# A graph layer on one core: aggregation by seven products on 2x2 blocks instead of eight

## The chip, the core and the metric

The kernel runs on one NeuronCore of a Trainium2 chip. The core has five engines with a queue each: TensorE (PE in the profile, with its weight loads listed apart as PEld), VectorE (DVE), ScalarE (ACT), GpSimd (POOL) and SyncE (SP), which here only starts transfers. Data lies in HBM, in the on-chip memory SBUF (128 partitions) and in PSUM, which TensorE writes and which this kernel uses as eight banks of 128x512 float32. The metric is the device time of the whole kernel in microseconds (us), the median of the runs. Everything is float32.

## The reference, cut to what matters

The layer takes 32 graphs of 512 nodes ("tokens") with 256 channels and a 0/1 adjacency matrix for each. After a layer norm and a relu, each graph goes through two branches (a convolution over the tokens and a message passing) and a GRU gate. The change is in one line of the message passing, the product of the affinities `A` (512 x 512) with the messages `msg` (512 x 256):

```python
h = jnp.maximum(_layernorm(x, axis=-1), 0.0)          # the x below
s = x @ w_se.T + b_se                                 # 3 features of a node
sq = jnp.sum(s * s, axis=-1)
dist = sq[:, :, None] + sq[:, None, :] - 2.0 * jnp.einsum('bnd,bmd->bnm', s, s)
A = jnp.exp(-dist) * mask                             # mask is the adjacency
msg = jax.nn.relu(x @ w_msg.T + b_msg)
x_nmp = jnp.einsum('bnm,bmd->bnd', A, msg)            # the aggregation
# x_conv: 1x1 convolution, relu, 17-tap convolution, relu
x_in = jnp.concatenate([x_conv, x_nmp], axis=-1)
gi, gh = x_in @ w_ih.T + b_ih, x @ w_hh.T + b_hh      # then r, z, n, and the output
```

## The kernel before

The 32 graphs are worked in two groups of 16. For each group a first part normalises the graphs and takes them to the frequency domain (the 17-tap convolution is done there). Then `nodes` does the message passing of the 16 graphs, and in between the frequency products of the convolution (`product`, 40 units in each group, three 128x256 products of two channel chunks for a unit). After both groups a late part does the inverse transforms and the gates, which already use a scheme of seven products.

The messages of one graph, and one unit of the convolution:

```python
    def message(b):
        MSG[b] = pools["nodes"].tile([P, NC, D], FP, tag="msg", name=f"msg_{b}", bufs=3)
        ST[b] = pools["nodes"].tile([P, 2, NC, NS], FP, tag="st", name=f"st_{b}", bufs=2)
        hq = HQ.pop(b)
        h = N // D
        for c0 in range(0, NC, h):
            m = MSG[b][:, c0 : c0 + h, :]
            for j in range(h):
                c = c0 + j
                p = bank(f"pm_{b}_{c}")
                for ic in range(DC):
                    nc.tensor.matmul(p[:, : D + NS], hq[:, ic, c * P : (c + 1) * P], wmsg[:, ic, :],
                                     start=(ic == 0), stop=(ic == DC - 1))
                nc.vector.tensor_add(ST[b][:, 0, c, :], p[:, D : D + NS], bmsg[:, D:])
                nc.vector.tensor_add(m[:, j, :], p[:, :D], bmsg[:, :D])
            nc.scalar.activation(m, m, AF.Relu)
...
    def product(pw, g, u, xf):
        if u > 0 and (g, u) not in BOTH or (g, u) not in WT:
            prepare(pw, g, u, xf)
        wt = WT.pop((g, u))
        re, im = factors_of(xf, u)
        wr, wi = wt[:, 0], wt[:, 1]

        y = pw.tile([P, 2, D], FP, tag="y", name=f"y_{g}_{u}", bufs=3)
        p = bank(f"py_{g}_{u}")
        k1, k2 = p[:, :D], p[:, D:]
        if u == 0:
            terms = [(k1, re, wr), (k2, im, wi)]
        else:
            both, wsum = BOTH.pop((g, u)), WSUM.pop((g, u))
            k3 = bank(f"py2_{g}_{u}")[:, :D]
            terms = [(k3, both[:, 1], wr), (k2, both[:, 0], wi), (k1, re, wsum)]
        for dst, v, w in terms:
            for ic in range(DC):
                nc.tensor.matmul(dst, v[:, ic, :], w[:, ic, :], start=(ic == 0), stop=(ic == DC - 1))
        y_re, y_im = (by_half(y[:, k, :]) for k in range(2))
        if u == 0:
            nc.scalar.copy(y_re, halves(k1))
            nc.scalar.copy(y_im, halves(k2))
        else:
            nc.scalar.copy(y_im, halves(k1))
            nc.vector.tensor_sub(y_re, y_im, halves(k2))
            nc.vector.tensor_add(y_im, y_im, halves(k3))
        nc.scalar.dma_start(YD[g][:, 2 * u : 2 * u + 2, :], y)
```

The affinities and the aggregation. `ADJ` is turned in 32x32 blocks on VectorE; `A[b][:, mc, :]` is the chunk `mc` of 128 neighbours by 512 nodes. `aggregate` makes two outputs of 128 channels by 512 nodes, four matmuls each:

```python
    def affinity(b):

        A[b] = pools["nodes"].tile([P, NC, N], FP, tag="A", name=f"A_{b}", bufs=2)
        sl, sr = SL.pop(b), SR.pop(b)
        pd = [bank(f"pd_{b}_{mc}") for mc in range(NC)]
        for mc in range(NC):
            rows = slice(32 * mc, 32 * mc + 3 * NS)
            nc.tensor.matmul(pd[mc], sl[rows, :], sr[rows, :], start=True, stop=True)
        for mc in range(NC):
            e = pools["nodes"].tile([P, N], FP, tag="e", name=f"e_{b}_{mc}", bufs=2)
            nc.scalar.activation(e, pd[mc], AF.Exp)
            at = pools["nodes"].tile([P, N], FP, tag="at", name=f"at_{b}_{mc}", bufs=2)
            nc.vector.transpose(at.rearrange("p (j k) -> p j k", k=32), ADJ[b][:, :, 32 * mc : 32 * (mc + 1)])
            nc.vector.tensor_mul(A[b][:, mc, :], e, at)
        del ADJ[b]

    def aggregate(b, dcs=range(DC)):
        if 0 in dcs:
            NMP[b] = work.tile([P, DC, N], FP, tag="nmp", name=f"nmp_{b}")
        for dc in dcs:
            p = bank(f"pn_{b}_{dc}")
            for mc in range(NC):
                nc.tensor.matmul(p, MSG[b][:, mc, dc * P : (dc + 1) * P], A[b][:, mc, :],
                                 start=(mc == 0), stop=(mc == NC - 1))
            nc.scalar.copy(NMP[b][:, dc, :], p)
        if DC - 1 in dcs:
            del MSG[b], A[b]

    def save_nmp(b):
        nc.scalar.dma_start(ND[b], NMP.pop(b))
```

The loop over the graphs of a group. Outside the `manual_schedule` blocks a scheduler of the compiler decides the order on each engine from the order of recording and from the dependencies:

```python
        def nodes(g, xf, units, last):


            b1 = (g + 1) * GB
            todo = [b1 - 1] + list(range(g * GB, b1 - 1))
            def begin(i):
                if i < GB:
                    if todo[i] not in HQ:
                        by_chunks(todo[i])
                    message(todo[i])
                    features(todo[i])

            load_adj(todo[0])
            with tc.manual_schedule():
                begin(0)
                message(todo[1])
                factors(todo[0])
                features(todo[1])
            affinity(todo[0])
            for i, b in enumerate(todo):
                mine = spread(units, i, last) if i < last else []
                more = i + 1 < GB

                if g + 1 < NG and i == GB // 2:
                    load_x(b1)
                if g + 1 < NG and i == 3 * GB // 4:
                    statistics(b1)
                if i + 2 < GB and todo[i + 2] not in HT:
                    load_h(todo[i + 2])
                if more:
                    load_adj(todo[i + 1])
                    factors(todo[i + 1])

                parts = [range(DC)] if mine or not more else [[0], [1]]
                if len(parts) > 1:
                    aggregate(b, parts.pop(0))
                for u in mine[:1]:
                    product(pools["pw"], g, u, xf)
                begin(i + 2)
                if more:
                    affinity(todo[i + 1])
                for u in mine[1:2]:
                    product(pools["pw"], g, u, xf)
                aggregate(b, *parts)
                save_nmp(b)
                for u in mine[2:]:
                    product(pools["pw"], g, u, xf)
```

The beginning of the late part, which is recorded by hand: the loads of the first pair of graphs and of the combined gate weights go out from GpSimd's queue, and GpSimd then makes the sums of their blocks.

```python
    with phase("late"), phase("sw"), phase("ops", bufs=2), phase("work"), tc.manual_schedule():
        pairs = B // 2
        sw = pools["sw"].tile([P, K3, 7, 3, P], FP, name="sw")
        load_pair(0, nc.gpsimd)
        load_combined(sw, 0, 2)
        sums(HP[0], True)
        sums(NP[0], False)
        load_combined(sw, 2, 7)
        inverse(0)
        sums(CP[0], False)
...
def load_pair(p, queue=nc.sync):
    # yt, hp and np of the pair p: two hp loads, two yt loads, two np loads
def load_combined(sw, q0, q1):
    for k in range(K3):
        nc.gpsimd.dma_start(sw[:, k, q0:q1], WS[k][:, q0:q1])
```

## Time and profile before

| | us |
|---|---|
| device time, median of 3 runs | 1846.07 (1845.53 to 1846.49) |
| span of the profiled execution | 1848.1 |
| busy: PE / PEld / DVE / ACT / POOL | 1826.4 / 1089.0 / 1109.1 / 581.9 / 588.2 |
| aggregation matmuls (line 489), 512 records | 225.9 |
| products of affinity and mask on VectorE (line 480), 128 | 114.5 |
| frequency products (line 393), 952 records | 151.0 + 81.0 + 5.0 |
| messages (line 439), 512 records | 117.5 |

A line of the groups reads: source line, engine, operation, output<-inputs, shapes, count | time in which at least one of the group ran, mean of one in ns | idle time of the engine just before them, and what ended it. Matmuls overlap each other, so the mean of one (593 ns for 128x512) is longer than the distance between two; the distance is the busy time over the count. One float32 matmul leaves two records, so 512 records are 256 matmuls of the program. A line of the timeline reads: start, duration in us, engine, line, operation, names, shapes, count of merged instructions, and in brackets the idle time before it with what ended it. Times count from the start of the span.

### The profile page before, as it was taken

The numbers are of one execution on the slowest core, as the hardware profiler recorded it, in microseconds if no ns is written. First come the engines' busy times: TensorE is split into PE (matmuls) and PEld (weight loads), VectorE is DVE, ScalarE is ACT, GpSimd is POOL, SyncE is SP. The second block draws the span as 40 slices with busy tenths as digits, with TensorE's granted clock in tenths as the row PEclk, the third lists the DMA queues.
The fourth block names the chain that finished last, engine by engine and source line by source line (L and its number), as shares of the span: only waits on it lengthen the run. The fifth ranks groups of instructions, "written<-read, shape, count | busy, mean of one in ns | idle before, by whom it ended". The sixth has DMA issues, their size and how long they took to land.

```text
span 1848.1 us, 20105 instructions
## 1 busy us (share of the span) xinstructions
PE 1826.4 (99%) x6610; PEld 1089.0 (59%) x6610; DVE 1109.1 (60%) x2220; ACT 581.9 (31%) x1083; POOL 588.2 (32%) x572
## 2 busy tenths in 40 slices
PE   9999999999999999999999999999999999999998
PEld 6777666666888666665555554555455544555443
DVE  7775656554885555545266466655666466645666
ACT  4555434432335333333222221222122221222121
POOL 3331333333432344444422323133212322133221
PEclk9999999999999999999999999999999999999999
DMA  8999888875678887778421443234422442244312
GB/s 233 299 276 241 225 226 246 218 179 180 212 250 207 235 245 235 216 207 261 123 86 34 120 120 99 53 88 120 120 78 43 120 120 88 49 103 120 112 25 52
DMA packets 307452, 289.26 MB, mean 157 GB/s; under 512 B 148028, under 2 KB 237148, under 8 KB 306964
## 3 DMA queue, kind: packets, MB, share of 16 engines
q1 hardware_dynamic: 281300, 224.22, 46.0%
q10 hardware_dynamic: 19024, 38.68, 5.9%
q0 software_dynamic: 7024, 25.07, 4.8%
q8 instruction: 53, 0.87, 0.2%
q14 instruction: 51, 0.42, 0.1%
HBM read 191.50 MB, written 96.40 MB: 156 GB/s over the span
## 4 chain that ended last, share of the span: by engine, by line
PE 89%; DVE 4%; issue 3%; DMA 2%; POOL 1%; ACT 1%; SPq 0%; POOLq 0%; ACTq 0%; DVEq 0%
PE pg L597 29%; PE pn L597 14%; PE pn L489 11%; PE py L393 11%; PE pm L439 6%; PE pc L585 5%; PE pc L328 3%; PE px L343 3%; PE pw L256 2%; PE pd L474 2%; PE phT L312 1%; DMA w<-in_w_ihT_dram 1%; PE psr L463 1%; DVE stats L285 1%; DVE xn L304 1%
## 5 line engine op out<-in xcount | busy, mean ns | idle before, releaser
L489 PE MATMUL pn<-A,msg 128*128 128x512 f32 x512 | 225.9, 593 | 0.6 <-DVE A L480 0.6
L597 PE MATMUL pg<-hp,sw 128*128 128x512 f32 x434 | 221.8, 593 | 0.7 <-DVE rz L616 0.5
L597 PE MATMUL pg<-np,sw 128*128 128x512 f32 x434 | 221.6, 592 | 0.0
L597 PE MATMUL pg<-cp,sw 128*128 128x512 f32 x434 | 221.6, 592 | 0.0
L575 POOL TENSOR_TENSOR hp<-hp 128x512 f32<-128x512 f32 x64 | 81.3, 1280 | 413.0 <-DMA hp<-hd 234.6
L372 POOL TENSOR_TENSOR both<-xf 128x256 f32<-128x256 f32 x78 | 60.1, 771 | 329.1 <-PE py L393 297.5
L489 PEld LDWEIGHTS pn<-A,msg 128*128 128x128 f32 x512 | 97.2, 191 | 110.9 <-issue 105.7
L575 POOL TENSOR_TENSOR cp<-cp 128x512 f32<-128x512 f32 x64 | 80.4, 1267 | 229.8 <-ACT cp L591 228.6
L393 PE MATMUL py<-wt,both 128*128 128x256 f32 x624 | 151.0, 385 | 0.7 <-issue 0.7
L612 ACT ACTIVATE rz<-rz,brz 128x512 f32<-128x512 f32 x93 | 67.0, 721 | 260.2 <-DVE rz L616 260.2
L400 DVE TENSOR_TENSOR y<-y,py 128x256 f32<-128x256 f32 x78 | 31.8, 408 | 190.5 <-ACT y L399 185.8
L597 PEld LDWEIGHTS pg<-hp,sw 128*128 128x128 f32 x434 | 82.2, 190 | 104.8 <-issue 97.8
L597 PEld LDWEIGHTS pg<-cp,sw 128*128 128x128 f32 x434 | 82.5, 190 | 103.8 <-issue 103.8
L597 PEld LDWEIGHTS pg<-np,sw 128*128 128x128 f32 x434 | 82.5, 190 | 103.8 <-issue 103.8
L393 PEld LDWEIGHTS py<-wt,both 128*128 128x128 f32 x624 | 114.3, 190 | 43.2 <-issue 28.3
L480 DVE TENSOR_TENSOR A<-e,at 128x512 f32<-128x512 f32 x128 | 114.5, 933 | 36.9 <-ACT e L477 36.7
L359 POOL TENSOR_TENSOR wsum<-wt 128x512 f32<-128x512 f32 x78 | 109.1, 1399 | 51.8 <-DMA wt<-wd 39.1
L735 ACT ACTIVATE nt<-nt,vech 128x512 f32<-128x512 f32 x64 | 46.2, 722 | 235.8 <-DVE nt L734 235.8
L328 PE MATMUL pc<-w,hT 128*128 128x256 f32 x512 | 116.7, 381 | 1.6 <-DVE hT L316 1.6
L439 PE MATMUL pm<-wmsg,hq 128*128 128x259 f32 x512 | 117.5, 382 | 0.6 <-ACT sl L460 0.6
L597 PE MATMUL pn<-np,sw 128*128 128x512 f32 x224 | 114.4, 592 | 0.0
L597 PE MATMUL pn<-cp,sw 128*128 128x512 f32 x224 | 114.4, 592 | 0.0
(146 smaller groups left out, 2963.6 us busy)
## 6 DMA issues: line engine op xcount, KB each, us to landing
wt<-wd SPq DMA_DIRECT2D x160, 256.0 KB, 4.3
adj<-in_adj_dram SPq DMA_DIRECT2D x128, 256.0 KB, 5.4
wd<-wst SPq DMA_DIRECT2D x64, 320.0 KB, 5.3
yd<-y ACTq DMA_DIRECT2D x80, 256.0 KB, 4.3
yt<-yd SPq DMA_DIRECT2D x30, 640.0 KB, 7.5
hd<-hT SPq DMA_DIRECT2D x32, 512.0 KB, 4.4
nd<-nmp ACTq DMA_DIRECT2D x32, 512.0 KB, 4.0
xb<-in_x_dram SPq DMA_DIRECT2D x128, 128.0 KB, 3.8
```

Of the source, the lines that this page charges most:

```text
L328: nc.tensor.matmul(p[:, j, :], HT[b][:, ic, c * P : (c + 1) * P], w1[:, ic, :], start=(ic == 0), stop=(ic == DC - 1))
L343: nc.tensor.matmul(p[:, j * 2 * L : (j + 1) * 2 * L], H1[b][:, c0 + j, ic * P : (ic + 1) * P], fwd, start=True, stop=True)
L359: nc.gpsimd.tensor_tensor(t, WT[g, u][:, 0], WT[g, u][:, 1], op=ALU.add)
L372: nc.gpsimd.tensor_tensor(both[:, 0], re, im, op=ALU.add)
L393: nc.tensor.matmul(dst, v[:, ic, :], w[:, ic, :], start=(ic == 0), stop=(ic == DC - 1))
L439: nc.tensor.matmul(p[:, : D + NS], hq[:, ic, c * P : (c + 1) * P], wmsg[:, ic, :], start=(ic == 0), stop=(ic == DC - 1))
L480: nc.vector.tensor_mul(A[b][:, mc, :], e, at)
L489: nc.tensor.matmul(p, MSG[b][:, mc, dc * P : (dc + 1) * P], A[b][:, mc, :], start=(mc == 0), stop=(mc == NC - 1))
L575: nc.gpsimd.tensor_tensor(t[:, dst, :], t[:, a, :], t[:, b, :], op=sub)
L585: nc.tensor.matmul(bk[:, t0:t1], YT[p][j][:, c, oc * P : (oc + 1) * P], back[:, n : n + t1 - t0], start=(c == 0), stop=(c == len(spans) - ...
L597: nc.tensor.matmul(bk[:, t], sw[:, k, q, o, :], terms[k][q][:, t], start=(first and i == 0), stop=(i == len(ks) - 1), skip_group_check=True)
L612: nc.scalar.activation(rz[:, g, j, :], src, AF.Sigmoid, bias=brz[:, g : g + 1], scale=1.0)
```

## The change

The 512 neighbours, the 256 channels and the 512 nodes are each cut in two halves, so that one graph's aggregation is a product of 2x2 block matrices. Eight block products (each 128 channels by 256 neighbours by 256 nodes) become seven (Winograd's form of Strassen's scheme). For it four sums of message blocks are made on VectorE (`message_sums`, 128x256 each) and four sums of affinity blocks on GpSimd (`affinity_sums`, 128x512 each). Three PSUM banks gather the seven products; blocks that enter two outputs are copied out by ScalarE and added by VectorE. `aggregate` is now a generator in three pieces, between which other work of TensorE is recorded.

To make room in SBUF, the exponential goes straight into `A` (the tiles `e` are gone), and `at` and `sr` have one buffer instead of two. The load of the graph after next moves one step ahead, and at the start of a group the second half of one graph's messages moves behind the transposes of another. In the diff, `m[:, i, k]` is the block of messages with the half `i` of the channels and the half `k` of the neighbours, and `a[:, k, j]` the block of affinities with the half `k` of the neighbours and the half `j` of the nodes.

```diff
@@ -105,6 +105,7 @@
     def bank(name):
         return psum.tile([P, N], FP, tag="bank", name=name)
 
+    SM, TA = {}, {}
     X, ADJ, XN, HT, HQ, H1, MSG, A, NMP, ST, SL, SR = ({} for _ in range(12))
     XP, HP, NP, CP, YT, RZ, NT, OUT = ({} for _ in range(8))
 
@@ -425,12 +426,13 @@
             nc.scalar.copy(chunks(HQ[b][:, ic, :]), by_chunk(HT[b][:, ic, :]))
         del HT[b]
 
-    def message(b):
-        MSG[b] = pools["nodes"].tile([P, NC, D], FP, tag="msg", name=f"msg_{b}", bufs=3)
-        ST[b] = pools["nodes"].tile([P, 2, NC, NS], FP, tag="st", name=f"st_{b}", bufs=2)
-        hq = HQ.pop(b)
-        h = N // D
-        for c0 in range(0, NC, h):
+    def message(b, halves=range(2)):
+        if 0 in halves:
+            MSG[b] = pools["nodes"].tile([P, NC, D], FP, tag="msg", name=f"msg_{b}", bufs=3)
+            ST[b] = pools["nodes"].tile([P, 2, NC, NS], FP, tag="st", name=f"st_{b}", bufs=2)
+        hq = HQ[b]
+        h = NC // 2
+        for c0 in (h * k for k in halves):
             m = MSG[b][:, c0 : c0 + h, :]
             for j in range(h):
                 c = c0 + j
@@ -441,6 +443,8 @@
                 nc.vector.tensor_add(ST[b][:, 0, c, :], p[:, D : D + NS], bmsg[:, D:])
                 nc.vector.tensor_add(m[:, j, :], p[:, :D], bmsg[:, :D])
             nc.scalar.activation(m, m, AF.Relu)
+        if 1 in halves:
+            del HQ[b]
 
     def features(b):
 
@@ -461,7 +465,7 @@
         p = bank(f"psr_{b}")
         for c in range(NC):
             nc.tensor.transpose(p[:, c * P : (c + 1) * P], fr[:, c].rearrange("p g k -> p (g k)"), ident)
-        t = SR[b] = pools["nodes"].tile([P, N], FP, tag="sr", name=f"sr_{b}", bufs=2)
+        t = SR[b] = pools["nodes"].tile([P, N], FP, tag="sr", name=f"sr_{b}", bufs=1)
         nc.scalar.copy(by_chunk(t), chunks(p))
 
     def affinity(b):
@@ -473,24 +477,71 @@
             rows = slice(32 * mc, 32 * mc + 3 * NS)
             nc.tensor.matmul(pd[mc], sl[rows, :], sr[rows, :], start=True, stop=True)
         for mc in range(NC):
-            e = pools["nodes"].tile([P, N], FP, tag="e", name=f"e_{b}_{mc}", bufs=2)
-            nc.scalar.activation(e, pd[mc], AF.Exp)
-            at = pools["nodes"].tile([P, N], FP, tag="at", name=f"at_{b}_{mc}", bufs=2)
+            nc.scalar.activation(A[b][:, mc, :], pd[mc], AF.Exp)
+            at = pools["nodes"].tile([P, N], FP, tag="at", name=f"at_{b}_{mc}", bufs=1)
             nc.vector.transpose(at.rearrange("p (j k) -> p j k", k=32), ADJ[b][:, :, 32 * mc : 32 * (mc + 1)])
-            nc.vector.tensor_mul(A[b][:, mc, :], e, at)
+            nc.vector.tensor_mul(A[b][:, mc, :], A[b][:, mc, :], at)
         del ADJ[b]
 
-    def aggregate(b, dcs=range(DC)):
-        if 0 in dcs:
-            NMP[b] = work.tile([P, DC, N], FP, tag="nmp", name=f"nmp_{b}")
-        for dc in dcs:
-            p = bank(f"pn_{b}_{dc}")
-            for mc in range(NC):
-                nc.tensor.matmul(p, MSG[b][:, mc, dc * P : (dc + 1) * P], A[b][:, mc, :],
-                                 start=(mc == 0), stop=(mc == NC - 1))
-            nc.scalar.copy(NMP[b][:, dc, :], p)
-        if DC - 1 in dcs:
-            del MSG[b], A[b]
+
+
+
+    H2 = NC // 2
+
+    def message_sums(b):
+        m = MSG[b].rearrange("p (k c) (i d) -> p i k c d", k=2, i=DC)
+        (a11, a12), (a21, a22) = (m[:, 0, 0], m[:, 0, 1]), (m[:, 1, 0], m[:, 1, 1])
+        t = SM[b] = pools["nodes"].tile([P, 3, H2, P], FP, tag="sm", name=f"sm_{b}", bufs=1)
+        s1, s2, s4 = (t[:, k] for k in range(3))
+        nc.vector.tensor_add(s1, a21, a22)
+        nc.vector.tensor_sub(s2, s1, a11)
+        nc.vector.tensor_sub(a21, a11, a21)
+        nc.vector.tensor_sub(s4, a12, s2)
+
+    def affinity_sums(b):
+        m = A[b].rearrange("p (k c) (j n) -> p k j c n", k=2, j=2)
+        (b11, b12), (b21, b22) = (m[:, 0, 0], m[:, 0, 1]), (m[:, 1, 0], m[:, 1, 1])
+        t = TA[b] = pools["nodes"].tile([P, 3, H2, N // 2], FP, tag="ta", name=f"ta_{b}", bufs=1)
+        t1, t2, t4 = (t[:, k] for k in range(3))
+        sub = ALU.subtract
+        nc.gpsimd.tensor_tensor(t1, b12, b11, op=sub)
+        nc.gpsimd.tensor_tensor(t2, b22, t1, op=sub)
+        nc.gpsimd.tensor_tensor(b12, b22, b12, op=sub)
+        nc.gpsimd.tensor_tensor(t4, b21, t2, op=sub)
+
+    def aggregate(b):
+
+        m = MSG[b].rearrange("p (k c) (i d) -> p i k c d", k=2, i=DC)
+        a = A[b].rearrange("p (k c) (j n) -> p k j c n", k=2, j=2)
+        out = NMP[b] = work.tile([P, DC, N], FP, tag="nmp", name=f"nmp_{b}")
+        (s1, s2, s4), (t1, t2, t4) = ([t[:, k] for k in range(3)] for t in (SM[b], TA[b]))
+        lo, hi = slice(0, N // 2), slice(N // 2, N)
+
+        def into(bk, w, v, first):
+            for c in range(H2):
+                nc.tensor.matmul(bk[:, lo], w[:, c], v[:, c], start=(first and c == 0), stop=(c == H2 - 1), skip_group_check=True)
+
+        b1, b2, b3 = (bank(f"pn{k}_{b}") for k in range(3))
+
+        p1, u2, u3 = out[:, 1, lo], out[:, 0, hi], out[:, 1, hi]
+        into(b1, m[:, 0, 0], a[:, 0, 0], True)
+        nc.scalar.copy(p1, b1[:, lo])
+        into(b2, s2, t2, True)
+        nc.vector.tensor_add(u2, p1, b2[:, lo])
+        yield
+        into(b1, m[:, 0, 1], a[:, 1, 0], False)
+        nc.scalar.copy(out[:, 0, lo], b1[:, lo])
+        into(b2, m[:, 1, 0], a[:, 0, 1], False)
+        nc.vector.tensor_add(u3, p1, b2[:, lo])
+        into(b3, s1, t1, True)
+        nc.vector.tensor_add(out[:, 1, hi], u3, b3[:, lo])
+        yield
+        into(b2, m[:, 1, 1], t4, False)
+        nc.vector.tensor_add(out[:, 1, lo], p1, b2[:, lo])
+        into(b3, s4, a[:, 1, 1], False)
+        nc.vector.tensor_add(out[:, 0, hi], u2, b3[:, lo])
+        del MSG[b], A[b], SM[b], TA[b]
+        yield
 
     def save_nmp(b):
         nc.scalar.dma_start(ND[b], NMP.pop(b))
@@ -945,8 +996,9 @@
             load_adj(todo[0])
             with tc.manual_schedule():
                 begin(0)
-                message(todo[1])
+                message(todo[1], [0])
                 factors(todo[0])
+                message(todo[1], [1])
                 features(todo[1])
             affinity(todo[0])
             for i, b in enumerate(todo):
@@ -957,23 +1009,24 @@
                     load_x(b1)
                 if g + 1 < NG and i == 3 * GB // 4:
                     statistics(b1)
-                if i + 2 < GB and todo[i + 2] not in HT:
-                    load_h(todo[i + 2])
                 if more:
                     load_adj(todo[i + 1])
                     factors(todo[i + 1])
-
-                parts = [range(DC)] if mine or not more else [[0], [1]]
-                if len(parts) > 1:
-                    aggregate(b, parts.pop(0))
+                parts = aggregate(b)
+                message_sums(b)
+                affinity_sums(b)
                 for u in mine[:1]:
                     product(pools["pw"], g, u, xf)
                 begin(i + 2)
+                if i + 3 < GB:
+                    load_h(todo[i + 3])
+                next(parts)
                 if more:
                     affinity(todo[i + 1])
+                next(parts)
                 for u in mine[1:2]:
                     product(pools["pw"], g, u, xf)
-                aggregate(b, *parts)
+                next(parts)
                 save_nmp(b)
                 for u in mine[2:]:
                     product(pools["pw"], g, u, xf)
```

## The prediction

> **What bounds the kernel now.** I read the busy shares first, then the groups, then the timeline of TensorE in one loop of `nodes`, and last the other engines' timelines at the places where the change could make TensorE wait. From the page:
>
> ```profile
> span 1848.1 us, 20105 instructions
> PE 1826.4 (99%) x6610; PEld 1089.0 (59%) x6610; DVE 1109.1 (60%) x2220; ACT 581.9 (31%) x1083; POOL 588.2 (32%) x572
> ...
> PEclk9999999999999999999999999999999999999999
> ...
> L489 PE MATMUL pn<-A,msg 128*128 128x512 f32 x512 | 225.9, 593 | 0.6 <-DVE A L480 0.6
> ...
> L575 POOL TENSOR_TENSOR hp<-hp 128x512 f32<-128x512 f32 x64 | 81.3, 1280 | 413.0 <-DMA hp<-hd 234.6
> ```
>
> TensorE is busy 99% of the span at full clock, so every us of its work that goes is a us of the end, and every new wait of it is a us lost. The aggregation waited 0.6 us in all. Timeline of TensorE, one loop with three units:
>
> ```profile
> 741.40 7.03 PE L489 MATMUL pn<-A,msg 128*128 128x512 f32 x16
> 748.27 1.89 PE L393 MATMUL py<-wt,both 128*128 128x256 f32 x8
> 750.00 1.03 PE L393 MATMUL py<-wsum,xf 128*128 128x256 f32 x4
> 750.86 0.27 PE L458 MATMUL psl<-ident,fl 128*128 128x128 f32 x1
> ...
> 757.60 1.14 PE L474 MATMUL pd<-sr,sl 9*128 9x512 f32 x8
> ...
> 761.36 7.03 PE L489 MATMUL pn<-A,msg 128*128 128x512 f32 x16
> ```
>
> Starts matter here, not durations. Sixteen 512-column records take 748.27 - 741.40 = 6.87 us, 0.429 each; twelve 256-column records take 750.86 - 748.27 = 2.59 us, 0.216 each. So halving the columns costs next to nothing per record (0.432 for two against 0.429). A loop lasts 19.96 us without a gap. Busy time in such a stretch, columns as in the page (PE, PEld, DVE, ACT, POOL, clock, DMA share, GB/s):
>
> ```profile
> 780.00:800.00 20.00, 20.00 (x83) 13.65 (x83) 10.77 (x28) 7.44 (x16) 8.59 (x9) 1.00 0.77 221
> ```
>
> VectorE has 9 us of room in 20, GpSimd 11.
>
> **What the Trainium skill says.** (1) "TensorE: Matmul & The Clock Gate", Back-to-back issue gap, gives N/2.4 + 2.5 ns for N columns: 109 ns for 256 and 216 for 512. The 216 and 429 ns here are twice 108 and 215, so one record holds two passes; the trace agrees. (2) The same page, Part 2, has matmuls stay in program order, only weight loads being pulled ahead, and calls GpSimd's queue a strict FIFO. So order decides what waits; the transfers that GpSimd issues stand between its sums in the trace, in order (below). (3) "GPSIMD Engine Reference", Engine selection: two-input elementwise work is about 2x slower than on VectorE. Here 128x512 takes 1.28 us (line 575) against 0.69 on VectorE (line 786). (4) The same page, Specifications: its SBUF interface is shared with VectorE, with contention when VectorE has two SBUF inputs. GpSimd's timeline agrees: the first pair below overlaps VectorE's affinity products, the second doesn't.
>
> ```profile
> 740.85 0.96 POOL L372 TENSOR_TENSOR both<-xf 128x256 f32<-128x256 f32 x1 [3.81 <-PE py L393]
> 742.46 1.71 POOL L359 TENSOR_TENSOR wsum<-wt 128x512 f32<-128x512 f32 x1
> 750.31 0.73 POOL L372 TENSOR_TENSOR both<-xf 128x256 f32<-128x256 f32 x1 [6.14 <-PE py L393]
> 751.68 1.27 POOL L359 TENSOR_TENSOR wsum<-wt 128x512 f32<-128x512 f32 x1
> ```
>
> **The change part by part.** *TensorE's work.* Before: 32 graphs x 16 records = 512 x 0.429 = 219.6 us. After: seven products of two chunks, two records each, 28 a graph: 896 x 0.216 = 193.5. Gain 26.1 us, 0.82 a graph. That is 1.4% of the time and the ceiling of the idea.
>
> *Steady loops.* I laid one loop out by hand from TensorE's order in the built program: affinity distances of the next graph (1.07 us), products 3 to 5, a unit (2.6), products 6 and 7, units and messages, then products 1 and 2 of the next graph. Affinities of the next graph are whole some 6 to 7 us after the distances (four exponentials at 0.6 on ScalarE, four turns at 0.65 and four products at 0.69 on VectorE). GpSimd then makes its four sums at 1.3, the second done about 11 us after the distances; TensorE asks for that one after 15 us in a loop with two units and 18 with three. VectorE gets four sums and five additions of 128x256 at about 0.42 (lines 400 and 401): 10.8 + 3.8 = 14.6 us of 19.1. GpSimd gets 5.1 to 6.8: at most 15.4 of 19.1. The longer chain inside the generator (the addition that frees bank 2 before product 6) falls about 1 us before TensorE wants it. I charge 0.1 us for each of 27 loops: +2.5.
>
> *Gaps that go.* TensorE stands 1.34 us at the start of each group while ScalarE copies `sr`; the moved half of the messages fills it. Three gaps of 1.54, 0.71 and 0.60 us by the distances, where banks wait for the two `e` tiles, should mostly go too, since the exponential no longer waits for a tile. -4.
>
> *Start of the groups.* Before, one graph's distances and a unit stood between the first affinities and their use. In the new order the first products follow the messages at once. Start of the first group before (TensorE and VectorE):
>
> ```profile
> 174.68 1.33 PE L474 MATMUL pd<-sr,sl 9*128 9x512 f32 x8 [1.34 <-ACT sr L465]
> ...
> 184.47 1.29 DVE L479 STREAM_TRANSPOSE at<-adj 128x512 f32<-128x512 f32 x2
> ...
> 187.31 7.03 PE L489 MATMUL pn<-A,msg 128*128 128x512 f32 x16
> ```
>
> VectorE turns the first adjacency only at 184.47 (now about 183), after the additions of the third graph's messages. Four turns and products take 5.4 us, to 188.5, and the second sum of GpSimd 1.3 more. TensorE would have been there at about 184: +6 for the first group; in the second the adjacency is turned earlier, +1.5. In the first group's second loop, GpSimd's queue has the four affinity sums ahead of the weight sum of unit 4, which TensorE wants about 3.5 us before it can be there: +3.5. Together +11.
>
> *End of the second group.* Its last three graphs have no units between. Products 6 and 7 then wait for VectorE, which has to finish three affinity chunks first, and the next graph's GpSimd sums start only when they are done (the sums have one buffer): I count about 4 us over two loops.
>
> *The way into the late part.* GpSimd's timeline before:
>
> ```profile
> 853.97 0.76 POOL L547 DMA_DIRECT2D hp<-hd  x1 [10.24 <-PE psr L463]
> ...
> 865.66 1.47 POOL L552 DMA_DIRECT2D np<-nd  x2 [8.41 <-issue]
> 867.12 1.63 POOL L539 DMA_DIRECT2D sw<-ws  x3
> 868.77 6.04 POOL L575 TENSOR_TENSOR hp<-hp 128x512 f32<-128x512 f32 x4
> 875.56 5.50 POOL L575 TENSOR_TENSOR np<-np 128x512 f32<-128x512 f32 x4 [0.76 <-DMA np<-nd]
> 881.00 1.61 POOL L539 DMA_DIRECT2D sw<-ws  x3
> ```
>
> These ran 28 us ahead of the first inverse transform, at 881.8, because GpSimd had no more work in the group. Now the affinity sums of the last three graphs stand before them in the same queue, and the last is done only some 2 us before TensorE ends the group. The transfers then start cold: `yt` takes 8.3 us to land, `np` 8.7, `sw` 8.5 to 9.7, and eight block sums of 1.28 us follow before the second half of `sw` is even asked for. TensorE has 5.7 us of inverse transforms and 10.3 us of products 1 and 2 to lay over this. Taken one after the other I get 6 us before the inverse and 4 to 9 in the gates: +10, between 5 and 15.
>
> Sum: -26.1 + 2.5 - 4 + 11 + 4 + 10 = -2.6, so 1843.5 us.
>
> **The rivals.** (a) *The clean gain*: waits as small as before, 1846 - 26 - 4 = about 1817. For it: nine us of VectorE and eleven of GpSimd free in each loop, and an order that puts other work between the pieces. Against it: the queue order at the two starts and above all at the way into the late part. (b) *VectorE or GpSimd becomes the bound* in the loops: contention on the shared SBUF interface (1.71 against 1.27 us above) lengthens both sets of sums, and VectorE's strict order then delays the additions that free the banks. Half a us a loop would give 1858, one us 1870. Against it: 4 us of room a loop on either engine. (c) *256-column records cost more than 0.216*, because a weight load of 0.190 hides under less: 0.230 would take 12.5 us. Against it: twelve records in 2.59 us, already with a new weight each. (d) *The late part's loads are hidden*: if the transfers land early enough, up to 10 us of my sum go, 1834.
>
> **Range and chances.** The ceiling of -26.1 - 4 bounds the good side at about 1816, 1.6% below, so faster by over 2% needs something I don't see: 0.03. Slower by over 2% means 37 us, more than a us and a half of waits a graph beyond my sum; rival (b) could do that: 0.07. The two waits I am least sure of, the late part (5 to 15) and the loops (0 to 15), give 1827 to 1860 for 8 in 10.
>
> **What the profile will show.** The aggregation should have 896 records starting 0.216 us apart, in all about 194 us. Loops with three units should last about 19.1 us and not 19.96. VectorE should be near 14.6 us in 20 of them. TensorE should stand about 6 us before the first group's second product, waiting for GpSimd or VectorE, and about 6 before the first inverse transform, waiting for `yt`, with more before the first products of the gates. If loops last over 19.5 us, the engines' room was misjudged; if TensorE has no gap at the late part, the queue order was; if the time is under 1825, both waits were too large in my sum.

## The result, and the profile after it

The changed kernel takes 1908.74 us (median of 4 executions, 1906.89 to 1912.75) against 1846.27 us before (1845.53 to 1846.49): a ratio of 1.0342, 95% interval 1.0324 to 1.0360. It is slower by 3.4%, far outside the range of 1827 to 1860 us. The head of the page, then TensorE's groups of the aggregation (busy us, mean ns of one, idle us before and what ended it):

```profile
span 1904.7 us, 21332 instructions
PE 1835.5 (96%) x6994; PEld 1166.8 (61%) x6994; DVE 1302.6 (68%) x2508; ACT 561.6 (29%) x1083; POOL 760.4 (40%) x700
...
PEclk9999899999999899999899999999999999999999
```

```profile
L522 PE MATMUL pn<-A,msg 128*128 128x256 f32 x384 | 103.6, 403 | 12.7 <-DVE A L483 7.2 <-ACT nmp L528 3.7 <-DVE nmp L530 1.2
L522 PE MATMUL pn<-ta,sm 128*128 128x256 f32 x256 | 70.3, 400 | 3.4 <-DVE sm L497 2.9 <-POOL ta L508 0.5
L522 PE MATMUL pn<-ta,msg 128*128 128x256 f32 x128 | 37.1, 414 | 12.1 <-DVE nmp L535 11.5
L522 PE MATMUL pn<-A,sm 128*128 128x256 f32 x128 | 36.5, 409 | 6.0 <-DVE nmp L537 6.0
```

The 896 records are there, and the aggregation, which waited 0.6 us before, now waits 34 us by itself. It waits for four different things: affinities (`A`), sums (`sm`, `ta`), the copies of line 528, and above all the additions that free PSUM banks (lines 530 to 537). The clock of TensorE has dips in three slices that it did not have.

Where the time went, by the starts of the distances (`pd`) of each graph, worked out from the trace:

| stretch | before | after | difference | the prediction's sum for it |
|---|---|---|---|---|
| first group's start, graphs 1 to 4 | 65.8 | 81.9 | +16.1 | |
| second group's start, graphs 1 to 4 | 69.2 | 83.4 | +14.2 | both starts +0.4 (11 - 4 - 8 x 0.82) |
| 11 loops of the first group | 195.3 | 197.7 | +2.4 | |
| 9 loops of the second group | 179.6 | 181.5 | +1.9 | 20 loops -14.4 (20 x -0.72) |
| 30th graph's distances to the end | 1010.7 | 1033.0 | +22.4 | about +11.5 (4 + 10 - 3 x 0.82) |

The rest differs by -0.2 us. Together these are the 56.6 us between the two profiled executions (1904.7 and 1848.1 us); the medians lie 62.5 us apart. All three parts of the sum failed, in the same direction.

*The loop.* TensorE in one loop of three units after the change:

```profile
690.17 1.14 PE L478 MATMUL pd<-sr,sl 9*128 9x512 f32 x8
691.25 1.99 PE L522 MATMUL pn<-A,msg 128*128 128x256 f32 x8
693.08 1.03 PE L522 MATMUL pn<-ta,sm 128*128 128x256 f32 x4
693.94 1.89 PE L394 MATMUL py<-wt,both 128*128 128x256 f32 x8
695.67 1.03 PE L394 MATMUL py<-wsum,xf 128*128 128x256 f32 x4
696.91 1.13 PE L522 MATMUL pn<-ta,msg 128*128 128x256 f32 x4 [0.21 <-DVE nmp L535]
698.32 1.13 PE L522 MATMUL pn<-A,sm 128*128 128x256 f32 x4 [0.28 <-DVE nmp L537]
...
710.35 1.14 PE L478 MATMUL pd<-sr,sl 9*128 9x512 f32 x8
```

The loop lasts 710.35 - 690.17 = 20.17 us: not 19.1 as predicted, and 0.21 more than before. Twelve records of a unit still take 2.59 us where nothing waits. But from the last unit's weight sums (695.67) to product 6 (696.91) it is 1.24 us for four records worth 0.86, and from product 6 to product 7 it is 1.41 for 0.86. The brackets show only 0.21 and 0.28 of this, because the ends of matmuls are modelled; the starts show all of it, 0.38 + 0.55, and 0.1 more behind it. The products themselves are not dear. Products 6 and 7 wait for VectorE, whose timeline at that place is:

```profile
695.11 0.69 DVE L483 TENSOR_TENSOR A<-A,at 128x512 f32<-128x512 f32 x1
695.84 0.71 DVE L482 STREAM_TRANSPOSE at<-adj 128x512 f32<-128x512 f32 x1
696.47 0.38 DVE L535 TENSOR_TENSOR nmp<-nmp,pn 128x256 f32<-128x256 f32 x1
696.78 1.16 DVE L483 TENSOR_TENSOR A<-A,at 128x512 f32<-128x512 f32 x1
697.86 0.41 DVE L537 TENSOR_TENSOR nmp<-nmp,pn 128x256 f32<-128x256 f32 x1
```

The first addition stands behind three affinity chunks of the next graph (the third is shown), and the fourth chunk, of 1.16 us, stands between the two. VectorE has time left in the loop (17.08 us busy of 20 here), and still TensorE waits for it: it is the order, not the sum, that counts.

*The start of the first group*, TensorE, and then the same stretch in windows (PE, PEld, DVE, ACT, POOL, granted clock, DMA share, GB/s):

```profile
184.11 0.67 PE L522 MATMUL pn<-A,msg 128*128 128x256 f32 x2 [2.49 <-DVE A L483]
185.56 1.22 PE L522 MATMUL pn<-A,msg 128*128 128x256 f32 x2 [0.78 <-DVE A L483]
...
230.46 2.08 PE L394 MATMUL py<-wsum,xf 128*128 128x256 f32 x4 [3.96 <-POOL wsum L360]
```

```profile
185.00:190.00 5.00, 3.42 (x6) 1.51 (x6) 3.66 (x5) 0.37 (x1) 2.19 (x2) 0.55 0.58 147
190.00:195.00 5.00, 4.82 (x14) 2.19 (x14) 0.42 (x1) 0.86 (x2) 2.79 (x3) 0.50 1.23 207
195.00:200.00 5.00, 5.00 (x15) 4.05 (x14) 1.72 (x4) 2.60 (x6) 0.00 (x0) 0.58 0.48 179
```

The wait for the affinities and the 3.96 us for the weight sum of unit 4 were predicted. What was not is the clock: behind the gaps it is at 0.50 to 0.58 in three windows of 5 us. Taken on TensorE's busy time in them, that costs 3.42 x 0.45 + 4.82 x 0.50 + 5.00 x 0.42 = 6.0 us more, so these gaps are paid twice. The kernel before shows the same on a small scale, behind the gap of 1.34 us at its first distances:

```profile
175.00:180.00 5.00, 5.00 (x22) 3.69 (x18) 0.00 (x0) 1.83 (x4) 1.27 (x1) 0.66 1.24 195
```

The prediction's "full clock" was read from the page, whose slices of 46 us print 9 for that. Summed in this way over the trace's record of the clock, from the first distances to 960 us, half clock costs 22.6 us after the change and 3.4 before. So 19 of the 56.6 us are clock: 5.9 at the first start, 6.7 at the second, 6.6 in the last stretch, and none in the loops. The Trainium skill, "TensorE: Matmul & The Clock Gate", Part 1 (The HAM clock gate), describes a half-rate state after an idle window of about 3.4 us. The half rate agrees; here gaps of 2.49 and 0.8 us with two records between them were enough.

*The way into the late part.* GpSimd, and what TensorE then waits for:

```profile
919.39 1.45 POOL L510 TENSOR_TENSOR ta<-A,ta 128x512 f32<-128x512 f32 x1
920.78 0.76 POOL L598 DMA_DIRECT2D hp<-hd  x1
```

```profile
928.83 4.77 PE L636 MATMUL pc<-back,yt 128*128 128x136 f32 x20 [3.22 <-DMA yt<-yd]
...
939.49 1.73 PE L648 MATMUL pg<-hp,sw 128*128 128x512 f32 x2 [2.55 <-DMA sw<-ws]
```

The loads start right behind the last affinity sum, 8 us ahead of the first inverse transform (928.83 - 920.78) instead of 28. That step was seen; its size is tested below.

### The profile page after: what moved, and what is told of

Same layout as the page of the kernel before. It is cut to its first block, busy times and chain, and to the rows that moved or that the text cites. A ratio compares the mean times of both kernels' runs of the same rounds, so it can differ in the third digit from the quotient of the medians.

```text
span 1904.7 us, 21332 instructions
## 1 busy us (share of the span) xinstructions
PE 1835.5 (96%) x6994; PEld 1166.8 (61%) x6994; DVE 1302.6 (68%) x2508; ACT 561.6 (29%) x1083; POOL 760.4 (40%) x700
## 4 chain that ended last, share of the span: by engine, by line
PE 56%; DVE 5%; issue 3%; POOL 2%; DMA 1%; ACT 1%; POOLq 0%; DVEq 0%
PE pg L648 28%; PE pn L648 14%; PE pc L636 4%; PE py L394 3%; PE pn L522 3%; PE pm L441 2%; DVE A L483 2%; DVE at L482 2%; PE pd L478 1%; DMA np<-nd 1%; DMA sw<-ws 1%; ACT A L480 0%; PE psr L467 0%; DVE nmp L537 0%; POOL np L626 0%
## 5 line engine op out<-in xcount | busy, mean ns | idle before, releaser
L626 POOL TENSOR_TENSOR cp<-cp 128x512 f32<-128x512 f32 x64 | 80.6, 1270 | 225.0 <-ACT cp L642 223.7
L394 PEld LDWEIGHTS py<-wt,both 128*128 128x128 f32 x624 | 117.8, 192 | 15.6 <-POOL both L374 0.3
L483 DVE TENSOR_TENSOR A<-A,at 128x512 f32<-128x512 f32 x128 | 100.8, 788 | 30.2 <-ACT A L480 22.8
L522 PE MATMUL pn<-A,msg 128*128 128x256 f32 x384 | 103.6, 403 | 12.7 <-DVE A L483 7.2
L648 PE MATMUL pn<-hp,sw 128*128 128x512 f32 x224 | 114.4, 592 | 0.0
L441 PEld LDWEIGHTS pm<-wmsg,hq 128*128 128x128 f32 x512 | 98.1, 193 | 15.9 <-ACT hq L426 0.5
```

The lines of the kernel that those rows point to most:

```text
L483: nc.vector.tensor_mul(A[b][:, mc, :], A[b][:, mc, :], at)
L522: nc.tensor.matmul(bk[:, lo], w[:, c], v[:, c], start=(first and c == 0), stop=(c == H2 - 1), skip_group_check=True)
L626: nc.gpsimd.tensor_tensor(t[:, dst, :], t[:, a, :], t[:, b, :], op=sub)
L648: nc.tensor.matmul(bk[:, t], sw[:, k, q, o, :], terms[k][q][:, t], start=(first and i == 0), stop=(i == len(ks) - 1), skip_group_check=True)
```

## The experiments

Theories at the outset. *Order on VectorE:* additions behind affinity chunks take the loops' gain. *Contention:* VectorE's message sums take 1.3 to 1.5 us each beside GpSimd's affinity sums instead of 0.42, and fill VectorE. *Queue on GpSimd:* affinity sums stand ahead of weight sums and loads. *Starts:* first products wait for affinities, and the clock drops.

In the table, medians and stretches in us as above ("loop" is one of three units in the second group; a range where they differ), with the ratio to the kernel before. In the first three rows of experiments part of the computation is left out. Medians of the kernel before differ by up to 3.4 us between the groups of runs, so small differences are read from the ratios.

| run | median | ratio, 95% interval | 1st start | 2nd start | loop | last stretch |
|---|---|---|---|---|---|---|
| before | 1846.3 | | 65.8 | 69.2 | 19.96 | 1010.7 |
| after | 1908.7 | 1.0342 (1.0324-1.0360) | 81.9 | 83.4 | 20.17 | 1033.0 |
| e1 no affinity sums | 1875.2 | 1.0170 (1.0155-1.0185) | 71.9 | 77.7 | 20.17 | 1017.4 |
| e2 no message sums | 1892.9 | 1.0264 (1.0248-1.0279) | 76.1 | 80.2 | 20.17 | 1034.2 |
| e3 no sums | 1868.0 | 1.0125 (1.0108-1.0142) | 72.9 | 75.8 | 20.17 | 1016.1 |
| e4 loads on SyncE | 1894.7 | 1.0280 (1.0258-1.0303) | 80.6 | 83.4 | 20.17 | 1020.0 |
| e5 third unit early | 1911.2 | 1.0345 (1.0315-1.0374) | 84.1 | 82.9 | 19.14-24.4 | 1036.4 |
| e6 five before distances | 2004.8 | 1.0850 (1.0832-1.0868) | 92.5 | 90.9 | 22.5-24.5 | 1033.8 |
| e7 eight at the ends | 1864.4 | 1.0086 (1.0069-1.0103) | 74.1 | 71.9 | 20.17 | 1009.3 |
| e8 e4 + e5 + e7 | 1864.2 | 1.0084 (1.0065-1.0103) | 73.5 | 70.5 | 19.14-22.0 | 1009.1 |
| e9 e5, sums on GpSimd | 1905.4 | 1.0329 (1.0295-1.0364) | 81.0 | 82.0 | 19.14-21.2 | 1031.5 |
| e10 e8 + e9, eight for three at each start | 1863.6 | 1.0097 (1.0067-1.0128) | 71.6 | 71.3 | 19.14-22.8 | 1009.3 |
| e11 sums ahead, units together | 1908.6 | 1.0328 (1.0312-1.0345) | 69.0 | 68.3 | 24.2-25.8 | 1011.3 |
| e12 second group only | 1849.1 | 1.0011 (1.0002-1.0020) | 63.5 | 71.1 | 20.50 | 1010.0 |
| e13 third `both` | 1840.7 | 0.9962 (0.9949-0.9974) | 62.7 | 71.1 | 19.1-20.0 | 1010.7 |
| e14 both groups | 1869.1 | 1.0114 (1.0099-1.0130) | 71.4 | 71.4 | 19.1-20.4 | 1008.5 |
| e15 eight everywhere | 1844.0 | 0.9990 (0.9981-0.9998) | 62.3 | 69.2 | 19.96 | 1011.1 |
| e16 product 5 before 4 | 1835.0 | 0.9941 (0.9920-0.9963) | 62.7 | 71.1 | 19.14 | 1008.5 |

### Taking the sums away: e1, e2, e3

e1 and e3 drop `affinity_sums(b)`, e2 and e3 drop `message_sums(b)`; the products read blocks instead, so the outputs are not the reference's:

```
-  (s1, s2, s4), (t1, t2, t4) = ... SM[b], TA[b]
+  t1, t2, t4 = a[:, 0, 1], a[:, 1, 1], a[:, 1, 0]      # e1, e3
+  s1, s2, s4 = m[:, 1, 0], m[:, 1, 1], m[:, 0, 1]      # e2, e3
```

> Leaves out GpSimd's four affinity sums of every graph (products 2, 5 and 6 read blocks of the affinities themselves), so the output is not the reference's. If contention between the two sets of sums is what eats the loops: VectorE's message sums fall from 1.3-1.5 us to about 0.45, VectorE gains some 3.5 us a loop, and the loop of three units falls from 20.17 to about 19.4 us; with the queue gaps gone too, about 1865 us. If GpSimd's queue order is the cost of the starts and of the way into the late part only: the two 4 us gaps before the products with wsum go and the last stretch falls by 12 to 15 us, but the loop stays at 20.0-20.2: 1882 to 1888 us. If VectorE's own order (additions standing behind affinity chunks) is what eats the loops, the loop stays at 20.0-20.2 here as well.

> Leaves out VectorE's four message sums (products 2, 4, 5 and 7 read blocks of the messages themselves), so the output is not the reference's. VectorE loses about 5.5 us of work a loop. If VectorE's load (sums lengthened by contention) is what eats the loops: loop of three units about 19.3 us, and the starts shorter by 2 to 3 us each; 1875 to 1885 us in all. If VectorE's order (exponentials, turns and products of affinities between the additions) eats them: the loop stays at 20.0 or above, and the total above 1895 us. The last stretch should hardly change (GpSimd's queue is as it was).

> Leaves out both sets of sums: seven products and their five additions and two copies alone; the output is not the reference's. If the sums are the whole cost: loop of three units 19.1-19.3 us and about 1830 us, the gain first predicted for TensorE. If the order on VectorE eats the loops: 19.9-20.1 us a loop of three units, still with waits for the additions before products 6 and 7, and the total at 1855 to 1870 us.

Measured: 1875.2, 1892.9 and 1868.0 us. The first two totals fall between the ranges given for their cases, so it is the loop that decides: with three units it stays at 20.17 us in all three runs, to 10 ns, even with no sum at all. In e3, TensorE and VectorE:

```profile
678.96 1.13 PE L523 MATMUL pn<-A,msg 128*128 128x256 f32 x4 [0.15 <-DVE nmp L536]
680.44 1.13 PE L523 MATMUL pn<-A,msg 128*128 128x256 f32 x4 [0.34 <-DVE nmp L538]
```

```profile
678.52 0.38 DVE L536 TENSOR_TENSOR nmp<-nmp,pn 128x256 f32<-128x256 f32 x1
678.83 1.22 DVE L483 TENSOR_TENSOR A<-A,at 128x512 f32<-128x512 f32 x1
679.98 0.41 DVE L538 TENSOR_TENSOR nmp<-nmp,pn 128x256 f32<-128x256 f32 x1
```

The same additions at the same place. So contention does not set the changed kernel's loop: that theory falls there, though the contention is real (group means of VectorE's four sums are 0.65, 1.31, 1.42 and 1.32 us, and in e1, without the affinity sums beside them, 0.46, 0.51, 0.50 and 0.69). The affinity sums cost at the ends: without them the starts are 10.0 and 5.7 us shorter and the last stretch 15.6. But the second start is still 6.6 us longer than before in e3, without sums: its trace has gaps of 0.84 and 1.14 us there, in wait for affinities, and half clock for 6.8 us behind them.

### The loads off GpSimd's queue: e4

```
-  load_pair(0, nc.gpsimd)                       # and nc.gpsimd in load_combined
+  load_pair(0, nc.sync)                         # and nc.sync
```

> Only the queue of the late part's first loads changes: SyncE issues them in place of GpSimd, where they stood behind the affinity sums of the last three graphs. If that queue is the cost of the way into the late part: the stretch from the last graph's distances to the end falls by 8 to 14 us, total 1895 to 1901 us. If the stretch is long because the three last graphs have no units and because the first inverse transform waits for the sums of hp and np: less than 3 us, 1905 to 1908 us. Loops unchanged in both.

Measured: 1894.7 us, last stretch 13.0 us shorter. The queue theory holds for 13 of the 22.4 us; the other 9.3 lie in the three graphs without units, where e4's trace still has 9.3 us of gaps and half clock for 6.8 us.

### More time for the additions: e5 and e6

```
e5   next(parts)                          e6   next(parts)
-    for u in mine[1:2]: product(...)     -    affinity(todo[i + 1])
+    for u in mine[1:]: product(...)           next(parts)
     next(parts)                          +    affinity(todo[i + 1])
```

> All sums stay; only the order of TensorE's work in loops with three units changes: the third unit goes ahead of products 6 and 7 instead of behind them, so that VectorE has 2.6 us more for the two additions that free banks 2 and 3. If those additions, standing behind affinity chunks in VectorE's order, are what takes the gain of the loops: loops of three units fall from 20.17 to 19.1-19.3 us, loops of two units stay at 17.58, total 1892 to 1897 us. If the loss is a fixed cost of seven products wherever they stand (hand-over of banks, semaphores): loops stay at 20.0-20.2 and the total within 3 us of 1908.

> All sums stay; products 3 to 5 go ahead of the next graph's distances instead of behind them, so that the additions of products 4 and 5 come ahead of the affinity chunks in VectorE's order. If that order takes the gain: loops of three units 19.2-19.5 us and of two units 16.6-17.0 us (a short wait of 0.2 us before product 4 remains, whose bank the first addition frees), total 1883 to 1893 us. If the fixed cost of seven products does: 20.0-20.2 and 17.5. If the affinities, now whole 1.3 to 2.6 us later, become the new bound: loops of two units above 17.6 us with waits for affinity sums, loops of three units at 19.2-19.5.

In e5 the loop over `mine[2:]` behind products 6 and 7 goes too. Four loops of the second group last 19.14 to 19.19 us, as the theory of order has it. The others last 19.6 to 24.4, and the total is no better. In the worst loop VectorE's message sums took 1.05 to 1.48 us each beside GpSimd's; the additions of the messages came late, their ReLU on ScalarE with them, and behind it in ScalarE's order the copy of product 1. TensorE there:

```profile
797.70 2.33 PE L478 MATMUL pd<-sr,sl 9*128 9x512 f32 x8
801.32 3.78 PE L522 MATMUL pn<-A,msg 128*128 128x256 f32 x8 [1.29 <-ACT nmp L528]
804.90 1.91 PE L522 MATMUL pn<-ta,sm 128*128 128x256 f32 x4
```

A gap of 1.29 us right behind the distances, and the eight records that follow take 3.58 us to the next start where eight at full clock take 1.73: half speed again.

e6 missed by far, with 2004.8 us. Products 3 to 5 now follow products 1 and 2 at once, and TensorE stands for the copy of product 1 (line 528), which frees bank 1: 2.11 us in a loop of 22.75. The distances had covered it. The order before had a use that I had not seen.

### The ends: e7 and e8

e7 takes eight products for graphs 1 and 2 of each group and the last three of the second:

```
+  old = i < 2 or (not mine)
+  if not old: parts = aggregate(b); message_sums(b); affinity_sums(b)
...
+  if old: aggregate_eight(b)        # as before: 16 records of 512 columns, two copies
+  else: next(parts)
```

> The first two graphs of each group and the last three of the second are aggregated by eight products, in the place and with the copies of the kernel before, without sums; all others by seven. If the starts and the way into the late part lose their time to waits for affinities, to sums ahead of other work in GpSimd's queue, and to the lower clock after such waits: start of the first group back from 82 to 66-68 us, of the second from 83 to 69-72, last stretch down by 14 to 20 us, total 1857 to 1870 us, loops as they were (20.17). If the starts lose it to the new order of loads and tiles (one tile for the turned adjacency, earlier load of h): less than half of the two starts comes back, total above 1878 us.

> Eight products for the first two graphs of each group and the last three of the second, late loads issued by SyncE, and the third unit ahead of products 6 and 7. If the three causes (VectorE's order in the loops, GpSimd's queue at the end, waits at the starts) are separate and add up: 1843 to 1856 us, loops of three units 19.1-19.3, loops of two still 17.58. If they overlap or one was misread: above 1860 us.

e7: the total of 1864.4 us and the second start are as expected, but the first start stays at 74.1 us instead of 66 to 68. The last stretch is even 1.4 us below that of the kernel before, with GpSimd still issuing the loads. So both the queue and the waits of the last graphs come from seven products where no unit stands between. The first start gave back 7.8 of 16.1 us, the second 11.5 of 14.2. e8 should have given 1843 to 1856 and stayed at 1864.2: the loads had nothing left to give, and e5's order scattered the loops again.

### The sums on GpSimd: e9 and e10

```
-  nc.vector.tensor_add(s1, a21, a22)            # and the three others
+  nc.gpsimd.tensor_tensor(s1, a21, a22, op=ALU.add)
```

> As e5 (third unit ahead of products 6 and 7), and the four message sums move from VectorE to GpSimd, three of them into its idle stretch behind the distances (0.73 us each when alone), the fourth ahead of the affinity sums. In e5 the loops fell to 19.14 us only in places: the later additions pushed the message sums of VectorE (1.3 to 1.5 us each beside GpSimd's sums) into the next messages, and the copy of product 1 came late, with a drop of the clock behind the gap. If that contention and load of VectorE is what spoils e5: loops of three units at 19.1-19.3 throughout, e5 minus 12 to 20 us, about 1891 to 1899 us. If GpSimd is then too full (16 us of 19): loops of 19.5 and more with waits for wsum, both or ta, total above 1905 us.

> As e9, with eight products for the first three graphs of each group and the last three of the second (no sums there), and the late part's first loads issued by SyncE. If the causes add up: start of the first group about 66-70 us, of the second about 69-71, last stretch about 1009, loops of three units 19.1-19.3, of two 17.4-17.6; total 1832 to 1845 us, at or below the kernel before. If GpSimd is too full in the loops: 1850 us or more.

Measured: 1905.4 and 1863.6 us: both miss. Of the nine loops only two last 19.14 us in either run, and others reach 22.8. VectorE at the start of a loop of 21.2 us in e10, and GpSimd beside it:

```profile
728.89 0.92 DVE L452 TENSOR_TENSOR st<-st 128x12 f32<-128x12 f32 x1
729.74 1.30 DVE L454 COPY fl<-st 128x12 f32<-128x12 f32 x1
730.95 0.79 DVE L456 TENSOR_SCALAR fr<-st 128x48 f32<-128x48 f32 x1
731.65 0.76 DVE L455 COPY fl<-st 128x12 f32<-128x12 f32 x1
732.32 1.33 DVE L457 TENSOR_SCALAR fr<-st 128x48 f32<-128x48 f32 x1
733.56 0.41 DVE L532 TENSOR_TENSOR nmp<-nmp,pn 128x256 f32<-128x256 f32 x1
```

```profile
729.74 1.27 POOL L512 TENSOR_TENSOR ta<-A,ta 128x512 f32<-128x512 f32 x1
730.96 0.73 POOL L373 TENSOR_TENSOR both<-xf 128x256 f32<-128x256 f32 x1
731.65 0.73 POOL L374 TENSOR_TENSOR both<-xf 128x256 f32<-128x256 f32 x1
732.33 1.26 POOL L360 TENSOR_TENSOR wsum<-wt 128x512 f32<-128x512 f32 x1
```

Copies of 12 elements take 0.16 us alone and 0.76 to 1.30 here, each as long as the GpSimd instruction beside it. Not the size counts but one GpSimd instruction for each of VectorE's. The addition (line 532), with one operand in PSUM, takes 0.41, as such additions do beside GpSimd's sums as well (mean 0.41 in the changed kernel's trace). This is where contention does set the loop: the five small operations put the first addition, and with it product 4, 2 us late. The cure is to have GpSimd's late sums elsewhere, not fewer of them.

### Sums ahead, and only where units are many: e11 to e14

From here the tiles of the sums are split, so that each is free as soon as its own product is done, and sums of the next graph are asked for right behind its distances. e11 also puts all units between products 5 and 6; e12 keeps seven products to graphs 4 to 13 of the second group:

```
+  if seven(i + 1): message_sums(todo[i + 1], 0); affinity_sums(todo[i + 1], 0)   # s1, s2, a21; t1, t2, b12
+  for u in mine[k0:k1]: product(...)            # e11: all units; e12: second and third
+  next(parts) if new else aggregate_eight(b)
```

> As e10, with the tile of the affinity sums split in three (each free as soon as its own product is done), three affinity sums of the next graph asked for right behind its affinities instead of a stretch later, and all units of a loop between products 5 and 6. In e10 loops lost 0.5 to 3.7 us where VectorE's small operations of the features (0.16 us alone) took 0.8 to 1.3 us each beside GpSimd's sums, and the first addition came late. If that lock-step of VectorE with GpSimd's late sums is the rest of the loss: loops of three units 19.1-19.3 and of two 16.5-16.9 us, total 1838 to 1852 us (the start of the first group still costs about 6). If it only moves to other operations: loops scatter as in e10, 1858 to 1868 us.

> Seven products only for graphs 4 to 13 of the second group, where a loop has three units; the whole first group and the others by eight. Three affinity sums ahead as in e11. If the start of the first group in e8 and e10 (71 to 74 us against 66) came from the sums of the third graph in GpSimd's queue: 65.5-67 us here, loops of the first group at 17.37 and 19.96, and 1836 to 1845 us in all. If it came from the new order of loads and tiles: 71 us or more here too, and about 1845 to 1853 us.

e11: loops of three units take 24.2 to 25.8 us. The third unit in a row waits for the sums of its parts, which stand in GpSimd's queue behind the affinity sums:

```profile
736.39 3.64 PE L394 MATMUL py<-wt,both 128*128 128x256 f32 x8 [3.37 <-POOL both L374]
```

The gap is followed by eight records in 3.47 us, half speed. But that part of its forecast which was for two units came true: of the first group's seven loops with two units, three last 16.55 us and three 16.90. TensorE in one of them, from distances to distances:

```profile
267.16 1.14 PE L478 MATMUL pd<-sr,sl 9*128 9x512 f32 x8
...
276.11 1.03 PE L526 MATMUL pn<-ta,msg 128*128 128x256 f32 x4
...
283.71 1.14 PE L478 MATMUL pd<-sr,sl 9*128 9x512 f32 x8
```

Product 6 (276.11) waits for nothing, and 16.55 us are 0.82 below the 17.37 of such a loop before. There both units stand between products 5 and 6. e12 is clean but for one such wait in each loop (1.10 us, again `both`), and gives 20.50 us. Its first start, with eight products and the new order of loads, is 63.5 us. So the 8 to 10 us more that e8 and e10 have there come from the first graphs with seven products, and not from the loads. In e8's trace a sum of the first such graph waits 9.42 us for its affinities ahead of a weight sum in GpSimd's queue, and TensorE then waits 4.26 us for that weight sum.

e13 mends the queue: a third buffer for `both`, and the sum of product 6 written over that of product 2, so that the next graph's sum for product 2 waits for product 6 and `both` goes ahead of it. The sums for products 6 and 7 are also asked for later, behind products 3 to 5. e14 does all this in both groups:

```
+  third = g == 1 and u % 3 == 0
+  both = (pools["nodes"] if third else pw).tile(..., bufs=1 if third else 2)
-  t4 = a tile of its own
+  nc.gpsimd.tensor_tensor(t2, b21, t2, op=sub)   # product 6's sum, in product 2's tile
```

> As e12 (seven products only for graphs 4 to 13 of the second group), with a third buffer for the parts' sums (both), and the affinity sum of product 6 written over that of product 2, so that GpSimd comes to the parts' sums before the affinity sums that are needed late. If GpSimd's queue order was the whole rest: loops of the second group 19.14-19.3 us in place of 20.50, total e12 minus 10 to 13 us, 1836 to 1840 us, and faster than the kernel before by about 0.4-0.5%. If the wait moves once more (to the additions, the features or the affinity sums of product 2): loops of 19.6-20.5 us and 1843 to 1852 us.

> As e13, with seven products also for graphs 4 to 16 of the first group, most of them in loops of two units. If two units leave GpSimd and VectorE enough time: loops of two units 16.6-17.0 us, start of the first group 66-68, total 1826 to 1836 us. If not (products 6 and 7 come only one unit behind the distances, and the sums of the first graphs stand ahead of the weight sums at the start): loops of 17.4-18 us, a start of 70 us or more, and 1840 us or more, so that the second group alone is the better version.

e13: 1840.7 us, loops mostly 19.6, with a total between those of its two cases: a wait for an addition ahead of product 4 (0.22 us in the bracket) is left. e14: 1869.1 us. In its loops of two units (18.3 to 20.4 us) product 6 comes one unit behind the distances and waits for the addition, 1.94 us in most, and the weight sum at the start costs 4.64 us again. One unit between products 5 and 6 is not enough cover; two were, in e11's loops of two units.

### What the products give: e15 and e16

e15 is the changed kernel with `aggregate_eight` for every graph and no sums. e16 is e13 with products 4 and 5 exchanged:

```
+  into(b3, s1, t1, True)                        # product 5 first
   into(b2, m[:, 1, 0], a[:, 0, 1], False)
   nc.vector.tensor_add(u3, p1, b2[:, lo])
-  into(b3, s1, t1, True)
```

> The changed kernel with eight products for every graph, in the order of the kernel before, and no sums; what stays of the change is the messages in two halves at the start of a group, the load of h a graph earlier and after other work, the affinity product in place and one tile for the turned adjacency. If e13's gain is mostly from these: first group's start about 62-63 us, second's about 70-71, loops 19.96 and 17.37, total 1840 to 1844 us. If these are neutral and the seven products gave it: 1845 to 1849 us.

> As e13, with product 5 ahead of product 4, which gives VectorE 0.43 us more for the addition that frees product 4's bank. If that wait is the rest of the loss in e13's loops: 19.2-19.3 us in place of 19.6, total 1836 to 1838.5 us. If the wait moves to the addition ahead of product 6 or elsewhere: 19.6 and 1839 to 1842 us.

e15: 1844.0 us, on the edge of its first case, but the ratio of 0.999 leaves only about 2 us for what else the change moved, against 0.9962 for e13. Its profile is 3.5 us shorter at the first start, where the kernel before has half clock for 6.8 us and e15 has none. So the seven products as placed by the change cost 1908.7 - 1844.0, about 65 us. e16: 1835.0 us, ratio 0.9941, faster than both and a little better than its forecast. TensorE in its loop:

```profile
690.22 1.14 PE L479 MATMUL pd<-sr,sl 9*128 9x512 f32 x8
691.29 1.13 PE L528 MATMUL pn<-A,msg 128*128 128x256 f32 x4
692.25 1.03 PE L528 MATMUL pn<-ta,sm 128*128 128x256 f32 x4
693.12 1.03 PE L528 MATMUL pn<-A,msg 128*128 128x256 f32 x4
...
699.16 1.03 PE L528 MATMUL pn<-ta,msg 128*128 128x256 f32 x4
700.02 1.03 PE L528 MATMUL pn<-A,sm 128*128 128x256 f32 x4
...
709.35 1.14 PE L479 MATMUL pd<-sr,sl 9*128 9x512 f32 x8
```

No bracket is left, and the loop is 709.35 - 690.22 = 19.13 us: 0.82 below the 19.96 before, all of the predicted gain of a graph. Over its ten graphs with seven products the distances come 8.2 us closer together than in e15, of the 9 us between the two medians.

## Why the prediction was wrong

- **TensorE's work, -26.1:** right. The records stand 0.216 us apart, and e16 shows the 0.82 us of a graph in full. The rival of dear 256-column records falls.
- **Steady loops, +2.5:** the step that failed most plainly, in its own term: 0.1 us a loop was charged and 1.03 was lost (20.17 against 19.14). The sentence that failed is "The longer chain inside the generator (the addition that frees bank 2 before product 6) falls about 1 us before TensorE wants it." I had summed VectorE's work (14.6 of 19.1 us) and not put the affinity chunks and the additions in VectorE's strict order; products 6 and 7 come one unit behind the distances, just when the chunks are being made. e1 to e3 show that the sums have no part in it, e5, e11 (two units) and e16 that the gain is there once the additions have time.
- **VectorE's sums at 0.42:** three times too small (1.31 to 1.42 us for three of the four) because GpSimd works beside them. Rival (b) named this, and its 1 us a loop is what the loops lost, but by another cause: that the size agrees is luck. Contention mattered only once the order was mended (e5, e10).
- **Gaps that go, -4, and the starts, +11:** net +0.4 was summed, with the gain of eight graphs in it, and 30.2 measured. The waits for affinities and for the weight sum of unit 4 were foreseen, 3.96 us against 3.5. In all, TensorE's gaps in the two starts grew by 16.5 us and the cost of half clock by 12.6. The gaps at the first distances of each group fell as foreseen, from 1.34 us to 0.77 and 0.17. Missing from the sum were the clock, which the prediction took to be full, and the same wait for a weight sum in the second group (4.04 us in the trace). e12 and e15 bring both starts back to 62-63 and 69-71 us.
- **End of the second group, +4, and the way into the late part, +10:** the mechanism was right and its size too small: the +22.4 and the 2.5 of gain that should have come off make some 25 us of loss against 14. The queue is 13.0 of them (e4), within the 5 to 15 given, though the prediction's own parts (6, and 4 to 9) add up to 10 to 15 and it charged the low end. The end of the group is about 12 (25 - 13) in place of 4 and was the mis-sized term: in e4's trace TensorE's gaps there, for additions, copies and sums, come to 9.3 us (2.78, 1.48, 2.46, 1.18 the longest), and half clock behind two of them costs 3.2 more.

That a transfer was hidden (d) or the gain clean (a) falls with the above. What stays open: how the starts' gaps divide between the order on VectorE and the sums, since each run that took one away moved the others too; why three of e11's loops of two units lose 0.35 us; and what e11's order in loops of two units gives together with e16's in loops of three, which was not tried.

## What to carry to other kernels

A product saved on the bounding engine is worth its time only where its new inputs and the new readers of its banks have work between them and it: put the additions that free a bank into the other engine's order by hand, with the times, before counting busy shares. Use the new form only in the stretch that has enough cover (here two units between products 5 and 6), and keep the old one at starts and ends, where sums are late and the longer gaps also cost clock. When a mended wait shows up elsewhere, look for the in-order queue it moved to; here it took three moves (additions, small operations, parts' sums) until the gain of 0.4% to 0.6% was there.

## What the runs showed of the hardware

- Beside GpSimd, a VectorE instruction that reads and writes SBUF alone takes about as long as the GpSimd instruction it meets: 0.76 to 1.33 us for copies and scalings of 12 to 48 elements that take 0.16 to 0.19 alone, and 1.3 to 1.5 us for sums of 256 elements that take 0.42. With an operand in PSUM (0.41) or as a 32x32 turn (0.71) it is not slowed. The Trainium skill, "GPSIMD Engine Reference", Specifications, names the contention and its kinds of instructions; the runs add that it is paid once an instruction, so that small ones suffer most.
- Gaps of TensorE were followed by half clock (records of 256 columns 0.427 us apart in place of 0.216) for 3.4, 6.8, 10.2 or 13.7 us. Not every gap was: in the 18 traces, between 60 and 1000 us, 43 of 128 gaps of 1 to 2 us had a stretch of half clock begin within 4 us behind them, and 67 of 69 gaps above 2.4 us. In the first group's start three gaps of 4.0 us together brought 6.0 us of clock.
- Behind a wait for another engine the first two records of 256 columns mostly stood 0.10 us further apart (0.32 in place of 0.216), before and after the change. The same gap stands behind the distances, where no wait is recorded, so its cause is not shown.
